# Where the steps of attention stand among the float16 and float32 passes of a gated block, and what follows them on the other engines

## The chip, the cores and the metric

The kernel runs on one core of a Trainium2 chip. The metric is the device time of the program in microseconds (us), as the median of several runs. TensorE (PE in the profile, its weight loads PEld), VectorE (DVE), ScalarE (ACT), GpSimd (POOL) and SyncE's DMA queue (SP) each work through a program of their own, in order, and wait for each other by semaphores.

## The reference

The input x has shape (8, 512, 256): eight batch elements of 512 tokens. After a layer norm, two branches read the same xn; the result is x + s * silu(f).

```python
x = L0_attn_query
xn = _layernorm(x, axis=-1)
s = _L0_attn_ref(xn, L0_attn_in_proj_w, L0_attn_out_proj_w)
g = _silu(_L0_ffn_ref(xn, L0_ffn_k0, L0_ffn_k1, L0_ffn_k2, L0_ffn_s0, L0_ffn_s1, L0_ffn_s2))
x = x + s * g
```

`_L0_attn_ref` has 16 heads of size 16: query, key and value projections, a rotary embedding of queries and keys, scores masked to the 250 latest positions (`(delta >= 0) & (delta < 250)`), softmax, values, and an output projection. `_L0_ffn_ref` has three layers whose weights are +1 or -1 (from booleans): [xn, -xn] of width 512 to 1024, relu and times 2, 1024 to 1024, relu and times 2, 1024 to 256. All of it is float32.

## The kernel before, in words

**Units.** The program handles the batch elements as eight units, b = 0 to 7, of T = 512 tokens in four tiles of 128. Work of neighbouring units overlaps: while unit b runs its feed-forward layers and its attention, unit b+1's norm, transposes (`turn_x`, tile `xnT_ps`) and key and query projections (`ka`, `kb`, `qa`, `qb`) are placed among them, and so are the third layer (`last`, `z_ps`) and the output projection of unit b-1.

**Two passes.** Each layer's product is made in two passes into one PSUM bank (`layer`, L396, matmuls L412): first "h", float16 weights and the float16 high part of the activations, then "l", float32 weights and the low part (`h1l`, `h2l`, type fp32r). Layer 1 is short (2 + 2 matmuls of 512 columns for each of 8 output tiles f), layer 2 long (8 + 8). ACT makes the high part with a relu (L423), DVE the low part from the PSUM bank (L421), and then the bank is free. In the last unit layer 2 is done in halves of 256 columns.

**Attention.** A unit's attention is nine steps (`steps`, L568, `step` and `attention`, L713). One step issues the score matmuls (`scores`, L598, each of 32 contraction rows), and behind them the value matmuls of the step before (`values`, L672, tile `po`). Between the two lie the exponentials on ACT, in two halves (L617), and the masks on POOL (`mask`, L633 and L640). When the heads of a group are complete, `keep` moves V and the sums S out of `po`: scalings on ACT for even groups (L692), additions on DVE for odd ones (L696). Group pairs are then divided: `invert` (DVE, reciprocals of S in four quarters, L742), `divide` (a DVE shuffle to R, L748, a product V*R on POOL, L751, and a count of unfit sums on POOL and DVE, L755 and L760).

**The end of a unit.** `gate_ready` (L492) makes 1/(1+exp(-z)): an exponential on ACT (L495), +1 on POOL (L498), a reciprocal on DVE (L502), a product on POOL (L503). `project_o` (L766) makes the output projection of tile t (`att_ps`, L770), issues the load of x's tile `xr` on SP (L775), multiplies by the gate on DVE (L783), adds xr on POOL and stores the result by a DMA on SP (L788, L789). `late` (L518) places `project_o`, and `gate_ready` comes 4 units of model time before it.

**What sets the order.** Everything is a list of pieces (time, cost, function). `run` (L209) sorts them by time and calls them; each may return followers with a delay, which go into a heap and are called when the sum of the costs so far has reached their due time. The order of the calls is the program order on every engine. The times are a model: SEQ = 42.0 for a unit, L1 = 0.87 for one f of layer 1, L2 = 3.45 for one f of layer 2, L3 = 1.87 for a tile of the third layer. The second exponential comes 0.3 after the first, the masks 1.2 after that, or at the latest when the next step needs them. `attention` places the nine steps: among the pieces of the unit, in order of time, it takes the first one at which at least n/9 of the unit's cost is done, and puts step n just ahead of it. Two pieces of one f of layer 2 (its h pass and its l pass) have times of their own, so a step can come to stand between the passes.

**PSUM.** Scores use 2 tiles of two banks, `po` one bank, and all else shares three banks (`ps_m`), which go round in program order. `probs`, the exponentials, has two buffers.

In a steady unit of the kernel before, TensorE's order is, with "sc po" for a step (scores of step n, values of step n-1) and h/l for the passes:

```
h1.0 v0 h1.1 v1 z0 sc1 po v2 v3 ... h1.5 z.2 sc2 po h1.6 h1.7 z.3 h2.0h sc3 po h2.0l xnT0 h2.1h xnT1 xnT2 h2.1l
sc4 po xnT3 h2.2h ka h2.2l kb sc5 po h2.3h qa qb h2.3l sc6 po h2.4h h2.4l att0 h2.5h sc7 po h2.5l att1
h2.6h h2.6l sc8 po att2 h2.7h h2.7l att3 sc0 po
```

Of the kernel before, what the change touches and what calls it, by code (L numbers as in the profile page):

```python
# [34 lines left out]
def tile_attention_times_gated_ffn(  # L35
# [39 lines left out]
    B, T, E = x.shape  # L75
# [123 lines left out]
    SEQ = 42.0  # L199
    L1, L2, L3 = 0.87, 3.45, 1.87  # L200
    states = {}

    def warm():

# [191 lines left out]
    def layer(b, name, src, w, f, part=0, parts_=1, cols=slice(0, T)):  # L396

        st = states[b]
        nc_in = w["l"].shape[1]
        if f == 0 and part == 0 and cols.start == 0:  # L400
            for p, dt in (("h", F16), ("l", F32R)):
                st[name + p] = hpool.tile(
                    [P, NF0, T], dt, tag=f"{name}{p}", name=f"{name}{p}_{b}"
                )
        if part == 0:
            st["h"] = ps_m.tile([P, T], F32, tag="mm", name=f"h_ps_{b}_{f}")
        ph = st["h"][:, cols]
        of_both = [(p, c) for p in "hl" for c in range(nc_in)]
        n = len(of_both)
        for k in range(n * part // parts_, n * (part + 1) // parts_):  # L410
            p, c = of_both[k]
            nc.tensor.matmul(  # L412
                ph, w[p][:, c, ts(f, P)], st[src + p][:, c, cols],
                start=(k == 0), stop=(k == n - 1),
            )
        if part + 1 < parts_:
            return
        hi, lo = (st[name + p][:, f, cols] for p in "hl")

        def low():  # L420
            nc.vector.scalar_tensor_tensor(lo, ph, 0.0, hi, ALU.max, ALU.subtract)  # L421

        high = lambda: nc.scalar.activation(hi, ph, AF.Relu)  # L423
        return [(0.0, high), (0.6 if f + 1 < NF0 else 0.0, low)]

    def last(b, t, how):
        st = states[b]
        pz = ps_m.tile([P, E], F32, tag="mm", name=f"z_ps_{b}_{t}")
        if how == "at once":
            for c in range(NF1):  # L430
                nc.tensor.matmul(
                    pz, st["h2p"][:, c, ts(t, P)], w2["l"][:, c].bitcast(F32),
                    start=(c == 0), stop=(c == NF1 - 1),
                )
        else:
            for p in "hl":
                for c in range(NF1):
                    nc.tensor.matmul(  # L438
                        pz, st["h2" + p][:, c, ts(t, P)], w2[p][:, c],
                        start=(c == 0 and p == "h"), stop=(c == NF1 - 1 and p == "l"),  # L440
                    )
        gate = st["gate", t] = outs.tile([P, E], F32, tag=f"gate{t}", name=f"gate_{b}_{t}")
        if how == "final":
            den = denominator(b, t)

            def ends():
                nc.scalar.activation(den, pz, AF.Exp, scale=scales[:, 1:2])
                nc.vector.scalar_tensor_tensor(
                    gate, pz, scales[:, 0:1], st["att", t], ALU.mult, ALU.mult
                )  # L450
                return [(0.5, add)]

            def add():
                nc.scalar.activation(den, den, AF.Identity, bias=1.0)
                return [(0.4, final)]

            def final():
                nc.vector.reciprocal(den, den)
                nc.vector.tensor_tensor(gate, gate, den, ALU.mult)
                nc.vector.tensor_tensor(gate, gate, st["xr", t], ALU.add)  # L460
                nc.sync.dma_start(out[b, ts(t, P), :], gate)

            return [(0.0, ends)]

        def scale():
            nc.vector.tensor_scalar(gate, pz, scales[:, 0:1], None, ALU.mult)
            if how != "later":
                return [(0.5, lambda: gate_ready(b, t))]

        return [(0.0, scale)]  # L470
# [40 lines left out]
    def last_at(b, t):  # L511

        if b + 1 < B:
            return SEQ * (b + 1) + 2 * L1 * (t + 1) + L3 * t
        half = t // 2
        return SEQ * b + NF0 * L1 + NT * L3 + HALF * (half + 1) - 2 * L3 + L3 * (t % 2)

    def late(b, t):  # L518

        if b + 1 == B:  # L520
            return SEQ * b + 40.0 + 0.9 * t
        return SEQ * (b + 1) + (31.0 + 3.5 * t if b + 2 < B else 18.0 + 2.5 * t)

    def finish_ffn(b, t, how):
        out = [(last_at(b, t), L3, lambda: last(b, t, how))]
        if how == "later":
            out.append((late(b, t) - 4.0, 0, lambda: gate_ready(b, t)))
        return out

    def ffn(b):  # L530

        now = SEQ * b + (NT * L3 if b == 0 else 0)
        out = []
        for f in range(NF0):
            out.append((now, L1, lambda f=f: layer(b, "h1", "x", w0, f)))
            now += L1
            if f % 2 and b > 0:
                now += L3
        if b + 1 == B:
            for half in range(2):  # L540
                cols = ts(half, T // 2)
                for f in range(NF1):
                    out.append((
                        now, L2 / 2,
                        lambda f=f, cols=cols: layer(b, "h2", "h1", w1, f, cols=cols),
                    ))
                    now += L2 / 2
                now += 2 * L3
            return out
        for f in range(NF1):  # L550
            for i in range(2):
                out.append(
                    (now, L2 / 2, lambda f=f, i=i: layer(b, "h2", "h1", w1, f, i, 2))
                )
                now += L2 / 2
        return out
# [11 lines left out]
    steps = [  # L568
        [(0, *whole_0), (0, *left_1)],
        [(0, *right_1), (0, *whole_2)],  # L570
        [(0, *whole_3), (1, *whole_0)],
        [(1, *whole_1), (1, *whole_3)],
        [(1, *whole_2), (2, *whole_2)],
        [(2, *whole_0), (2, *left_1)],
        [(2, *right_1), (2, *whole_3), (3, *whole_3)],
        [(3, *whole_0), (3, *left_1)],
# [5 lines left out]
    def once(f):  # L582

        calls = [f]
        return lambda: calls.pop()() if calls else None
# [23 lines left out]
    def exponentials(b, i, sc, n):  # L609
        p = probs.tile([P, 4, T], F32, tag="p", name=f"p_{b}_{i}")  # L610

        def exps():
            half_of(0)
            return [(0.3, second)]

        def half_of(half):
            nc.scalar.activation(  # L617
                p[:, 2 * half : 2 * half + 2, :n], sc[half][:, :, :n], AF.Exp,
                scale=D ** -0.5,
            )  # L620

        second = once(lambda: half_of(1) or [(1.2, masks)])
        masks = once(lambda: mask(i, p))
        return p, lambda: (second(), masks()), once(exps)

# [87 lines left out]
    def attention(b, among):  # L713

        first, end = SEQ * b + (20.6 if b == 0 else 0.0), ends_at(b)
        inside = sorted((at, cost) for at, cost, _ in among if first <= at < end)
        whole = sum(cost for _, cost in inside)
        times, done = [], 0.0
        for at, cost in inside:
            if len(times) < len(steps) and done * len(steps) >= whole * len(times):  # L720
                times.append(at - 0.01)
            done += cost
        out = []
        for n in range(len(steps)):
            out.append((times[n], 1.7, lambda n=n: step(b, n)))
        for g in range(NG):

            at = times[used[g - 2][-1]] + 0.01 if g > 1 else first - (10.0 if b else 2.0)
            if b and g == 1:
                at = first + 0.01  # L730
            out.append((at, 0, lambda g=g: stack(b, g)))
        if b + 1 == B:
            out.append((end, 0.7, flush))
        return out
# [65 lines left out]
    def divisions(b):  # L800
        out = []
        for pair in range(2):
            if b + 1 < B:
                first, d = (SEQ * b + 29.0, 2.0) if pair == 0 else (SEQ * (b + 1) + 4.2, 2.0)
            else:
                first, d = SEQ * b + (20.0 if pair == 0 else 30.6), 1.3
            for n in range(4):
                out.append((first + d * n, 0, lambda p=pair, n=n: invert(b, p, n)))
            out.append((first + d * 4, 0, lambda p=pair: divide(b, p)))
        return out  # L810

    whole = small.tile([1, 1], mybir.dt.int32, tag="whole", name="whole")
# [169 lines left out]
```

## Time and profile before

| what | value |
|---|---|
| median of three runs | 635.44 us (634.3 to 636.73) |
| the profiled execution | 636.03 us, span 634.3 us |
| granted TensorE clock, mean | 0.993 |
| TensorE busy | 612.7 us, 97% of the span |
| VectorE, GpSimd, ScalarE busy | 388.8, 312.3, 297.7 us |
| starts of units 0 to 7 on TensorE (first matmul of layer 1) | 19.03, 91.31, 166.61, 242.04, 317.33, 393.02, 468.59, 544.43 us |
| last matmul of the body | about 624.5 us |

The page has one line for each engine's busy time, a row of tenths for forty slices of the span, the chain of work that ended last, and groups of instructions by line. A timeline lists an engine's instructions by start, with their duration, and in brackets the engine's idle time ahead of one and what ended it. [...] a matmul group's bar reaches into the next one's; what a piece costs TensorE is read from its start to the next piece's start. A unit's period is the distance of two unit starts.

### The profile page before, as it was taken

How to read it: one execution, taken by the hardware profiler on the slowest of the kernel's cores; microseconds unless marked ns; L12 is line 12 of the kernel's file. 1: busy time of each engine (PE TensorE's matmuls, PEld its weight loads, DVE VectorE, ACT ScalarE, POOL GpSimd, SP SyncE). 2: the span in 40 equal slices, each digit the busy share in tenths (PEclk: the TensorE clock that was granted, in tenths of full speed). 3: DMA queues.
4: the chain of work that ended last, by engine and by line, in shares of the span. 5: the costliest groups of instructions: out<-in, count | busy, mean ns of one | idle time of the engine just before them, and what ended most of it. 6: DMA issues, size and time to landing. Idle time of an engine off the chain costs nothing.

```text
span 634.3 us, 12013 instructions
## 1 busy us (share of the span) xinstructions
PE 612.7 (97%) x4834; PEld 398.8 (63%) x4834; DVE 388.8 (61%) x668; ACT 297.7 (47%) x442; POOL 312.3 (49%) x406
## 2 busy tenths in 40 slices
PE   7899999999999999999999999999999999999993
PEld 5454567656766567655676566665666556768783
DVE  6584436656675475756657577665566557457564
ACT  3566564525444445444454454452545445464321
POOL 1935451455633557426544348145472346738630
PEclk9899999999999999999999999999999999999998
DMA  8263621215321153113431153311443115221101
GB/s 270 78 232 117 233 85 34 63 71 177 123 85 50 68 208 126 51 51 146 145 109 51 63 197 106 116 62 76 151 127 105 51 68 208 93 85 42 52 25 40
DMA packets 38194, 67.21 MB, mean 106 GB/s; under 512 B 5104, under 2 KB 19184, under 8 KB 38128
## 3 DMA queue, kind: packets, MB, share of 16 engines
q1 hardware_dynamic: 36384, 64.24, 29.7%
q10 hardware_dynamic: 1744, 2.10, 1.0%
q8 instruction: 40, 0.66, 0.4%
q14 instruction: 26, 0.21, 0.1%
HBM read 36.96 MB, written 29.36 MB: 105 GB/s over the span
## 4 chain that ended last, share of the span: by engine, by line
PE 70%; POOL 8%; DVE 6%; DMA 5%; ACT 5%; issue 3%; SPq 1%; POOLq 0%; ACTq 0%
PE h_ps L412 32%; PE z_ps L438 8%; PE po L672 8%; PE sc L598 6%; PE v_ps L289 4%; DMA xr<-in_x_dram 3%; PE att_ps L770 3%; ACT p L617 2%; DMA kb<-in_k_dram 2%; PE kb_ps L304 2%; PE ka_ps L304 2%; PE qb_ps L304 1%; PE qa_ps L304 1%; DVE den L502 1%; PE xnT_ps L265 1%
## 5 line engine op out<-in xcount | busy, mean ns | idle before, releaser
L617 ACT ACTIVATE p<-sc 128x1024 f32<-128x1024 f32 (+2 forms) x144 | 138.5, 1014 | 119.0 <-PE sc L598 80.9
L412 PE MATMUL h_ps<-h1l,w1l_sb 128*128 128x512 f32 (+1 forms) x576 | 143.1, 390 | 0.0
L633 POOL TENSOR_SCALAR_AFFINE_SELECT p<-p 128x512 f32<-128x512 f32 x128 | 88.0, 693 | 76.2 <-ACT p L617 76.1
L412 PE MATMUL h_ps<-h1h,w1h_sb 128*128 128x512 f16 (+1 forms) x576 | 122.8, 356 | 0.9 <-ACT v_pad L296 0.5
L412 PEld LDWEIGHTS h_ps<-h1l,w1l_sb 128*128 128x128 f32 x576 | 98.4, 188 | 27.6 <-issue 9.6
L423 ACT ACTIVATE h2h<-h_ps 128x512 f16<-128x512 f32 (+1 forms) x72 | 39.9, 554 | 113.8 <-PE h_ps L412 113.7
L412 PEld LDWEIGHTS <-w1h_sb 128*128 128x128 f16 x576 | 53.6, 98 | 52.3 <-issue 7.5
L672 PE MATMUL po<-p,v_pad 128*32 128x378 f32 (+4 forms) x1216 | 76.9, 372 | 1.7 <-POOL p L640 1.3
L502 DVE RECIPROCAL den<-den 128x256 f32<-128x256 f32 x30 | 52.2, 1739 | 41.5 <-POOL den L498 41.5
L421 DVE SCALAR_TENSOR_TENSOR h2l<-h_ps,h2h 128x512 fp32r<-128x512 f32 (+1 forms) x72 | 43.5, 605 | 43.0 <-ACT h2h L423 43.0
L640 POOL TENSOR_SCALAR_AFFINE_SELECT p<-p 128x512 f32<-128x512 f32 (+1 forms) x96 | 49.2, 512 | 41.2 <-ACT p L617 41.1
L421 DVE SCALAR_TENSOR_TENSOR h1l<-h_ps,h1h 128x512 fp32r<-128x512 f32 x64 | 42.6, 676 | 33.4 <-ACT h1h L423 33.1
L598 PEld LDWEIGHTS sc<-q,k 32*128 32x128 f32 x1216 | 44.0, 184 | 28.4 <-issue 18.8
L742 DVE RECIPROCAL S<-S 128x128 f32<-128x128 f32 x64 | 59.3, 934 | 0.0
L598 PE MATMUL sc<-q,k 32*128 32x378 f32 (+4 forms) x1216 | 57.1, 306 | 0.0
L412 PE MATMUL h_ps<-xl,w0l_sb 128*128 128x512 f32 x128 | 53.5, 500 | 0.0
L423 ACT ACTIVATE h1h<-h_ps 128x512 f16<-128x512 f32 x64 | 38.2, 597 | 32.6 <-PE h_ps L412 32.3
L672 PEld LDWEIGHTS po<-p,v_pad 128*32 128x32 f32 x1216 | 31.7, 109 | 30.7 <-issue 16.7
L788 POOL TENSOR_TENSOR gate<-gate,xr 128x256 f32<-128x256 f32 x30 | 22.0, 732 | 51.0 <-DMA xr<-in_x_dram 38.6
L412 PE MATMUL h_ps<-xh,w0h_sb 128*128 128x512 f16 x128 | 39.5, 391 | 0.6 <-DVE gate L783 0.5
L438 PE MATMUL z_ps<-w2l_sb,h2l 128*128 128x256 f32 x256 | 38.3, 291 | 0.5 <-DVE h2l L421 0.5
L336 POOL TENSOR_TENSOR m_ka<-m_ka,m_kb 128x512 f32<-128x512 f32 x16 | 20.1, 1278 | 34.3 <-DVE m_kb L316 31.8
(95 smaller groups left out, 809.5 us busy)
## 6 DMA issues: line engine op xcount, KB each, us to landing
q<-dq SPq DMA_DIRECT2D x64, 256.0 KB, 3.5
dq<-qh SPq DMA_DIRECT2D x16, 512.0 KB, 3.4
dq<-m_qa SPq DMA_DIRECT2D x16, 512.0 KB, 3.8
k<-dk SPq DMA_DIRECT2D x32, 256.0 KB, 2.7
dk<-kh SPq DMA_DIRECT2D x8, 512.0 KB, 2.6
dk<-m_ka SPq DMA_DIRECT2D x8, 512.0 KB, 2.6
xr<-in_x_dram SPq DMA_DIRECT2D x32, 128.0 KB, 2.9
out_dram<-gate SPq DMA_DIRECT2D x32, 128.0 KB, 1.7
```

Source lines behind the costliest of these rows:

```text
L304: nc.tensor.matmul(ps, wqkv_sb[:, c, ds(col, P)], st["xT"][:, c, :], start=(c == 0), stop=(c == EC - 1),)
L412: nc.tensor.matmul(ph, w[p][:, c, ts(f, P)], st[src + p][:, c, cols], start=(k == 0), stop=(k == n - 1),)
L421: nc.vector.scalar_tensor_tensor(lo, ph, 0.0, hi, ALU.max, ALU.subtract)
L423: high = lambda: nc.scalar.activation(hi, ph, AF.Relu)
L438: nc.tensor.matmul(pz, st["h2" + p][:, c, ts(t, P)], w2[p][:, c], start=(c == 0 and p == "h"), stop=(c == NF1 - 1 and p == "l"),)
L502: nc.vector.reciprocal(den, den)
L598: nc.tensor.matmul(sc[r // 2][:, r % 2, ds(off, n)], st["k0", g][row, ts(j, P)], st[f"q{turn}", g][row, ds(j * P + first, n)], start=(turn ...
L617: nc.scalar.activation(p[:, 2 * half : 2 * half + 2, :n], sc[half][:, :, :n], AF.Exp, scale=D ** -0.5,)
L633: nc.gpsimd.affine_select(out=block, in_=block, compare_op=ALU.is_ge, fill=0.0, base=0, pattern=[[0, 4], [1, P]], channel_multiplier=-1,)
L640: nc.gpsimd.affine_select(out=block, in_=block, compare_op=ALU.is_ge, fill=0.0, base=-1, pattern=[[0, 4], [-1, beyond]], channel_multiplier=1,
L672: nc.tensor.matmul(po[32 * r : 32 * r + 32, ds(j * P + first, n)], v_columns(j, g, r), p_[:, r, ds(off, n)], start=(j == 0), stop=(done an ...
L742: nc.vector.reciprocal(part, part)
```

## The change

Four edits, none of which adds or removes an instruction on any engine:

1. A set `quick` collects the times of the pieces whose first pass is float16: each third-layer tile, each f of layer 1, and each f of layer 2 as a whole (for the last unit each half of an f). `attention` now places step n ahead of that one of these pieces whose share of the unit's cost is nearest to n/9; each place is used once. In unit 0 every piece is allowed.
2. `late` for units 0 to 5 goes from 31.0 + 3.5 t to 32.0 + 3.2 t, for the output projections and, 4 earlier, `gate_ready`.
3. The masks follow the second exponential by 0.6 in place of 1.2.
4. The divisions of the first pair start at 30.0 in place of 29.0.

```diff
+    quick = set()
...
-        return SEQ * (b + 1) + (31.0 + 3.5 * t if b + 2 < B else 18.0 + 2.5 * t)
+        return SEQ * (b + 1) + (32.0 + 3.2 * t if b + 2 < B else 18.0 + 2.5 * t)
 
     def finish_ffn(b, t, how):
+        quick.add(last_at(b, t))
...
         for f in range(NF0):
+            quick.add(now)
             out.append((now, L1, lambda f=f: layer(b, "h1", "x", w0, f)))
...
                 for f in range(NF1):
+                    quick.add(now)
                     out.append((
                         now, L2 / 2,
                         lambda f=f, cols=cols: layer(b, "h2", "h1", w1, f, cols=cols),
...
         for f in range(NF1):
+            quick.add(now)
             for i in range(2):
                 out.append(
                     (now, L2 / 2, lambda f=f, i=i: layer(b, "h2", "h1", w1, f, i, 2))
...
-        second = once(lambda: half_of(1) or [(1.2, masks)])
+        second = once(lambda: half_of(1) or [(0.6, masks)])
...
         times, done = [], 0.0
+        places = {}
         for at, cost in inside:
-            if len(times) < len(steps) and done * len(steps) >= whole * len(times):
-                times.append(at - 0.01)
+            if at in quick or b == 0:
+                places[at] = done
             done += cost
+        for n in range(len(steps)):
+            at = min(places, key=lambda at: abs(places[at] * len(steps) - whole * n))
+            del places[at]
+            times.append(at - 0.01)
...
-                first, d = (SEQ * b + 29.0, 2.0) if pair == 0 else (SEQ * (b + 1) + 4.2, 2.0)
+                first, d = (SEQ * b + 30.0, 2.0) if pair == 0 else (SEQ * (b + 1) + 4.2, 2.0)
```

In a steady unit this gives, on TensorE:

```
h1.0 v0 h1.1 v1 z0 sc1 po v2 v3 ... h1.5 sc2 po z.2 h1.6 h1.7 z.3 sc3 po h2.0h h2.0l xnT0 h2.1h xnT1 xnT2 h2.1l
xnT3 sc4 po h2.2h ka h2.2l kb sc5 po h2.3h qa qb h2.3l sc6 po h2.4h h2.4l sc7 po h2.5h att0 h2.5l
h2.6h att1 h2.6l att2 sc8 po h2.7h h2.7l att3 sc0 po
```

Steps 2, 3, 4, 7 and 8 stand elsewhere, and the output projections of tiles 0 and 1 stand between the passes of h2.5 and h2.6. In the last unit steps 2 to 6 stand up to a piece earlier. POOL's order at the end of a unit changes from `den_2+1, gate_1+xr_1, gate_2*den_2, den_3+1, masks of step 8, gate_2+xr_2, V*R` to `den_2+1, gate_1+xr_1, gate_2*den_2, den_3+1, gate_2+xr_2, V*R, masks of step 8`, and on SP the loads of the next unit's first stack (one of k, two of q) stand ahead of the store of tile 0. In the last unit DVE's reciprocal of den_1 stands ahead of the V and S additions.

## The prediction

> **What bounds the kernel now.** I read the page first, then the windows by unit, then the timelines of TensorE and of all engines in units 2 and 3. The busy row and the chain that ended last:
>
> ```profile
> PE 612.7 (97%) x4834; PEld 398.8 (63%) x4834; DVE 388.8 (61%) x668; ACT 297.7 (47%) x442; POOL 312.3 (49%) x406
> ...
> PE 70%; POOL 8%; DVE 6%; DMA 5%; ACT 5%; issue 3%; SPq 1%; POOLq 0%; ACTq 0%
> ```
>
> TensorE is busy 97% of 634.3 us and no other engine above 61%. The units start at 19.03, 91.31, 166.61, 242.04, 317.33, 393.02, 468.59 and 544.43. Windows cut there (columns: length, then busy us and count of PE, weight loads, DVE, ACT, POOL, then granted clock, DMA share, GB/s):
>
> ```profile
> 242.04:317.33 75.29, 75.15 (x589) 47.89 (x585) 48.20 (x81) 35.26 (x53) 36.61 (x50) 1.00 0.32 105
> ...
> 544.43:634.30 89.87, 78.31 (x758) 62.63 (x754) 51.27 (x85) 35.55 (x62) 40.70 (x55) 0.97 0.18 55
> ```
>
> Units 1 to 6 are TensorE end to end: 453.1 us for six, the shortest 75.29. Only the order of TensorE's work, and short waits, can move them. "Busy" hides the second part, since the bars overlap, so I measured from start to start. TensorE in unit 2:
>
> ```profile
> 223.11 1.89 PE L412 MATMUL h_ps<-h1h,w1h_sb 128*128 128x512 f16 x8
> 224.93 0.79 PE L598 MATMUL sc<-q,k 32*128 32x378 f32 x16
> 225.65 0.84 PE L672 MATMUL po<-p,v_pad 128*32 128x244 f32 x16
> 226.42 2.14 PE L412 MATMUL h_ps<-h1l,w1l_sb 128*128 128x512 f32 x8
> 228.40 1.02 PE L770 MATMUL att_ps<-wo_sb,V 128*128 128x256 f32 x4
> 229.26 1.89 PE L412 MATMUL h_ps<-h1h,w1h_sb 128*128 128x512 f16 x8
> 230.79 2.21 PE L412 MATMUL h_ps<-h1l,w1l_sb 128*128 128x512 f32 x8
> 232.94 0.74 PE L598 MATMUL sc<-q,k 32*128 32x244 f32 x16
> ```
>
> An unbroken pair of passes followed by a step takes 232.94 − 229.26 = 3.68 us. The pair with step 7 inside takes 228.40 − 223.11 = 5.29, less 0.72 for scores and 0.77 for values = 3.80. A step inside a pair costs 0.12 more than one in front of a float16 pass.
>
> The third view is the only sizeable wait that repeats. All engines in unit 3, after step 3 (stood inside a pair):
>
> ```profile
> 266.55 1.92 ACT L617 ACTIVATE p<-sc 128x1012 f32<-128x1012 f32 x2 [3.78 <-PE sc L598]
> ...
> 269.49 0.62 ACT L423 ACTIVATE h2h<-h_ps 128x512 f16<-128x512 f32 x1
> ...
> 270.14 0.69 DVE L421 SCALAR_TENSOR_TENSOR h2l<-h_ps,h2h 128x512 fp32r<-128x512 f32 x1 [0.23 <-ACT h2h L423]
> ...
> 270.89 0.20 PEld L265 LDWEIGHTS xnT_ps<-ident,xn 128*128 128x128 f32 x2 [0.59 <-DVE h2l L421]
> ```
>
> ACT is in the exponentials of step 3 and two scalings when the layer-2 product ends, so the relu comes late, the residual on DVE after it, and the transpose that needs the PSUM bank waits. From h pass to transpose is 1.983 us here; without such a wait it is 1.727. Cost 0.26 a unit.
>
> [...] the page's weight-load groups show 98 ns for w1h (float16), 188 ns for w1l. [...] In the trace the long load is hidden after 512-column matmuls (an f16 pass to its l pass has no extra time), but not after values: from values to the second matmul of an l pass is 0.34 us against 0.23 elsewhere. [...] the relu stands behind exponentials.
>
> **The change part by part.** Instruction counts on each engine stay, so everything is order. PE, DVE and POOL programs were read in both versions.
>
> *Steps in steady units (1 to 6).* Steps 2, 3, 4, 7 and 8 move. Boundary prices, start to start: values before an l pass +0.11, before a transpose +0.055, before an output projection (att) +0.107 (0.968 against 0.861), before a float16 pass 0; before scores always about 0.10, whatever stands there. Step 2 moves from one float16 pass (h1) to another (z): 0. Step 3 leaves the inside of pair 0: −0.116. Step 4 moves from a transpose to h2.h2: −0.03 after small shifts. Step 7 leaves pair 5 and step 8 moves behind att 2: the stretch from step 7 to att 3 is 14.20 now; the pieces in the new order sum to 14.01: −0.19. Sum −0.34 a unit.
>
> *Output projection one unit of model time later.* Att 0 and 1 now stand inside pairs 5 and 6. The nearest row is the projection ka inside a pair: 200.86 to 206.16 is 5.30, which is an unbroken pair in front of att 3 (235.80 to 239.38, 3.58) plus qa's own advance (1.72). So a float32 piece there costs 0; bounds 0 and +0.11 each. I take 0, since the full-width load behind a 512-column matmul is hidden in that row.
>
> *Transpose wait.* Step 3 now ends a whole pair before the relu that it delayed, so ACT is free: −0.26 a unit (bounds 0 and −0.26). The stall could move to step 4, now before h2.h2, but that relu is one pair off: 0.
>
> *Small waits.* Six units at the floor of 75.20 would be 451.2, so 1.93 us are stray waits (the v copies and step-8 masks). I leave 1.2, or 0.2 a unit. Together: 6 × (−0.34 − 0.26) − 0.73 = −4.3.
>
> *Masks sooner, divisions later, and the queues.* POOL's order changes at each unit's end. Before:
>
> ```profile
> 312.69 0.73 POOL L788 TENSOR_TENSOR gate<-gate,xr 128x256 f32<-128x256 f32 x1 [3.39 <-DMA xr<-in_x_dram]
> ...
> 314.89 0.64 POOL L640 TENSOR_SCALAR_AFFINE_SELECT p<-p 128x512 f32<-128x512 f32 x1
> ```
>
> Step 8's masks stood behind the gate_1+xr_1 store and ended at 316.29, just when values needed them. After, they stand behind gate_2+xr_2 and V·R, too. On SP the three loads of the next unit's first stack go ahead of out_0, so xr_1 is issued about 304.6 (was 308.80). Then in unit 3: xr_1 lands 308.5, sum to 309.2, out_1, xr_2 issued 309.6, landed 312.0 (2.4, as for xr_2 before), sum 312.7, V·R (1.28) 314.0, masks (1.4) 315.4. Values want them at 316.0. Cover 0.6 us. I cost it at 0, but if xr_2 takes 3.9, as xr_1 did, it is +0.9 a unit. Mask of step 6 likewise: its exponentials end 295.8, den_0's exponential now stands ahead of them on ACT, masks end about 297.7, values at 298.4. Att 3's product, behind masks on POOL, is ready about 316.5 and its bank is wanted at 318.8.
>
> *Unit 0.* Steps 2, 3, 7, 8 move: −0.15. Scores to values of step 4 take 1.08 against 0.67 for lack of masks (0.4); these come 0.6 sooner: −0.35. Sum −0.5.
>
> *Last unit.* Waits now: 0.92 (step 8's values, 0.86 of it masks behind two gate sums), and about 1.6 around the z passes and flush (masks, h2l). After, steps 2 to 6 stand one piece sooner, and on DVE den_1's reciprocal (1.75) moves ahead of the V and S scalings that step 6's values need. In sequence: masks of step 4 from 569.2, V·R 1.28, den_0+1 0.85, reciprocal 1.75, product 0.74, den_1+1 0.85, reciprocal 1.75, V and S 1.5, so values at about 580.0 with TensorE there at 578.4: +1.6. Behind it, part of the later waits disappears (0.9 + 0.4, and transitions 0.3). Sum 0, bounds −1 and +1.5.
>
> *Sum.* −4.3 − 0.5 + 0 = −4.8 on the profiled execution's 636.03: 631.2. The median shown is 0.59 below it, so 630.6. Start and tail (19.0 us before unit 0, 9.7 after TensorE's last matmul) are left as they are.
>
> **Rivals.**
> *The likeliest* ends at 629.4 to 632.0: boundaries and the transpose pay, the rest nearly cancels.
> *Given back in part*: att inside pairs costs 0.1 each (+1.2 in six units), or the last unit shows its 1.5 in full: 632 to 634.5. For it: the DVE row den is 1.74 us[...]. Against: ka in a pair costs nothing.
> *More*: masks and xr stay early in the last unit and its 0.9 plus 0.9 fall away: 628 to 629.4. For it, POOL is 49% busy; against, den_1 on DVE.
> *Slower*: the POOL queue at the unit's end. If xr_2 lands 1.5 us or more later than I set (the page has 2.9 median, 5.6 at most), step 8's masks hold up step 0's values in seven units. Past the 0.6 cover it costs one for one; at 0.7 a unit the gain is gone, at 1.2 it is 639.0. For it: 38.6 us of POOL's idle time ended on xr. Against: out_0 and so xr_1 go sooner.
> *No effect*: pairs cost the same whatever they surround, the 0.12 being where records start; the transposes' wait moves to another bank: 635.
>
> **How the numbers follow.** The chances: likeliest 0.60, given back 0.18, more 0.12, slower 0.06, no effect 0.04. Half a per cent is 3.2 us, about what a measurement of this kernel can tell from no change: bounds 632.3 and 638.6. Faster: 0.60 + 0.12 + 0.04 of the second = 0.76. Same: 0.14 + 0.04 = 0.18. Slower 0.06. The range 628.0 to 634.2 takes in the first three but their ends and leaves out the last two.
>
> **What would show it.** Right: units 1 to 6 at 74.6 to 74.9; the pair with step 7 gone from TensorE's timeline and its pairs at 3.68 between att and scores; h pass to transpose 1 at 1.73, with the relu at its product's end. Wrong: TensorE idle on p from POOL L640 in front of step 0's values in steady units, with V·R or gate+xr ahead of the masks; values at 0.1 or more longer before att; units at 75.2; and a wait over 1.6 us at step 6 of the last unit.

## The result, and the profile after

The changed kernel takes 630.84 us as the median of four runs (630.22 to 632.4), the kernel before 635.39 (634.3 to 636.73) beside it: a ratio of 0.992, with a 95% interval of 0.990 to 0.9941. The forecast was 630.6. The profiled execution of the changed kernel took 632.4 us with a span of 630.6, so the two profiled executions differ by 3.6 us.

The busy row and the chain of work that ended last, of the changed kernel:

```profile
PE 609.6 (97%) x4834; PEld 398.8 (63%) x4834; DVE 393.0 (62%) x668; ACT 300.0 (48%) x442; POOL 316.1 (50%) x406
...
PE 84%; DVE 6%; DMA 4%; POOL 3%; ACT 2%; issue 1%; SPq 0%; POOLq 0%; ACTq 0%
```

TensorE is as busy as before, but its share of the last chain rose from 70% to 84%, and POOL's fell from 8% to 3%: fewer waits in front of TensorE end at POOL (its waits for masks fell from 1.3 us, in three, to 0.3, in two). The units start at 19.03, 90.63, 166.20, 241.24, 316.15, 391.06, 465.92 and 540.84, and the last matmul of the body ends at 620.31 (before: 624.54). Windows of the changed kernel for units 3 and 7 (columns as in the prediction: length, then busy us and count of PE, weight loads, DVE, ACT, POOL, then granted clock, DMA share, GB/s):

```profile
241.24:316.15 74.91, 74.77 (x588) 47.95 (x585) 48.85 (x82) 35.64 (x53) 38.66 (x51) 1.00 0.32 106
...
540.84:630.60 89.76, 77.91 (x758) 62.44 (x754) 51.07 (x84) 35.53 (x62) 39.87 (x54) 0.97 0.17 54
```

| stretch | before | after | difference | forecast |
|---|---|---|---|---|
| unit 0 | 72.28 | 71.60 | -0.68 | -0.5 |
| units 1 to 6, sum | 453.13 | 450.21 | -2.92 | -4.3 |
| unit 7, to the last matmul | 80.11 | 79.47 | -0.64 | 0 |
| after the last matmul | 9.76 | 10.29 | +0.53 | 0 |
| span | 634.3 | 630.6 | -3.7 | -4.8 |

TensorE in unit 2 of the changed kernel, at the place where step 7 stood inside a pair:

```profile
221.71 0.82 PE L605 MATMUL sc<-q,k 32*128 32x378 f32 x16
222.45 0.84 PE L679 MATMUL po<-p,v_pad 128*32 128x244 f32 x16
223.22 1.90 PE L415 MATMUL h_ps<-h1h,w1h_sb 128*128 128x512 f16 x8
224.96 1.03 PE L782 MATMUL att_ps<-wo_sb,V 128*128 128x256 f32 x4
225.63 2.21 PE L415 MATMUL h_ps<-h1l,w1l_sb 128*128 128x512 f32 x8
227.68 1.90 PE L415 MATMUL h_ps<-h1h,w1h_sb 128*128 128x512 f16 x8
```

The pair with att 0 inside takes 227.68 − 223.22 = 4.46 us, an unbroken pair's 3.58 plus 0.88. So the projection costs its own time there and nothing more, as forecast.

All engines of the changed kernel in unit 3, at the transpose that was forecast to lose its wait:

```profile
267.89 0.60 ACT L426 ACTIVATE h2h<-h_ps 128x512 f16<-128x512 f32 x1 [0.88 <-PE h_ps L415]
267.91 1.89 PE L415 MATMUL h_ps<-h1h,w1h_sb 128*128 128x512 f16 x8
268.11 0.42 DVE L280 COPY xT<-xnT_ps 128x256 f32<-128x256 f32 x1 [0.79 <-PE xnT_ps L268]
268.45 0.79 DVE L250 TENSOR_SCALAR xn<-x,mv,rstd 128x256 f32<-128x256 f32 x1
...
269.17 0.68 DVE L424 SCALAR_TENSOR_TENSOR h2l<-h_ps,h2h 128x512 fp32r<-128x512 f32 x1
...
269.90 0.20 PEld L268 LDWEIGHTS xnT_ps<-ident,xn 128*128 128x128 f32 x2 [0.59 <-DVE h2l L424]
```

ACT is now free and takes the relu as soon as the product ends, as forecast: in step with the next h pass, where it came 0.58 us behind it before. But the transpose still waits: 269.90 − 267.91 = 1.99 us, as before (1.98). The residual h2l could have started at the earliest when the relu ended, at 268.49. It starts at 269.17, because the norm of the next tile (0.79 us) stands ahead of it on DVE. It stood there before, too, where it ended ahead of the relu; the h pass and the norm of the kernel before:

```profile
268.91 1.89 PE L412 MATMUL h_ps<-h1h,w1h_sb 128*128 128x512 f16 x8
...
269.45 0.46 DVE L247 TENSOR_SCALAR xn<-x,mv,rstd 128x256 f32<-128x256 f32 x1
```

POOL of the changed kernel at the end of unit 3:

```profile
311.88 0.74 POOL L800 TENSOR_TENSOR gate<-gate,xr 128x256 f32<-128x256 f32 x1 [1.34 <-DMA xr<-in_x_dram]
312.58 1.28 POOL L763 TENSOR_TENSOR V<-V,R 128x512 f32<-128x512 f32 x1
313.81 0.64 POOL L647 TENSOR_SCALAR_AFFINE_SELECT p<-p 128x512 f32<-128x512 f32 x1
...
314.99 0.23 POOL L647 TENSOR_SCALAR_AFFINE_SELECT p<-p 128x24 f32<-128x24 f32 x1
```

Step 8's masks end at 315.22, and the values of step 0 start at 315.17. The forecast's times for this unit were on the clock of before, where the unit starts at 242.04; here it starts at 241.24. From the start of the unit the values come at 73.93 us (forecast 73.96), but the masks end at 73.98 (forecast 73.36). The cover of 0.6 us doesn't exist: the masks come just in time. In unit 1, where xr_2 came later, step 0's values waited, and scores to unit end took 0.58 us more (0.95 and 1.34 against 0.73 and 0.98).

### The profile page after: what moved, and what is told of

It reads as the page before. It is cut to its first block, busy times and chain, and to the rows that moved or that the text cites. A ratio compares the mean times of both kernels' runs of the same rounds, so it can differ in the third digit from the quotient of the medians.

```text
span 630.6 us, 12029 instructions
## 1 busy us (share of the span) xinstructions
PE 609.6 (97%) x4834; PEld 398.8 (63%) x4834; DVE 393.0 (62%) x668; ACT 300.0 (48%) x442; POOL 316.1 (50%) x406
## 4 chain that ended last, share of the span: by engine, by line
PE 84%; DVE 6%; DMA 4%; POOL 3%; ACT 2%; issue 1%; SPq 0%; POOLq 0%; ACTq 0%
PE h_ps L415 40%; PE po L679 11%; PE z_ps L441 9%; PE sc L605 7%; PE v_ps L292 4%; PE att_ps L782 4%; PE qa_ps L307 2%; PE kb_ps L307 2%; PE qb_ps L307 2%; DMA kb<-in_k_dram 2%; DMA xr<-in_x_dram 2%; PE ka_ps L307 2%; PE xnT_ps L268 1%; DVE den L505 1%; ACT p L624 1%
## 5 line engine op out<-in xcount | busy, mean ns | idle before, releaser
L640 POOL TENSOR_SCALAR_AFFINE_SELECT p<-p 128x512 f32<-128x512 f32 x128 | 93.8, 739 | 106.5 <-ACT p L624 106.5
L415 PEld LDWEIGHTS <-w1h_sb 128*128 128x128 f16 x576 | 51.6, 98 | 55.8 <-issue 14.0
```

Source lines behind the costliest of these rows:

```text
L415: nc.tensor.matmul(ph, w[p][:, c, ts(f, P)], st[src + p][:, c, cols], start=(k == 0), stop=(k == n - 1),)
L640: nc.gpsimd.affine_select(out=block, in_=block, compare_op=ALU.is_ge, fill=0.0, base=0, pattern=[[0, 4], [1, P]], channel_multiplier=-1,)
```

## The experiments

One table for all; units are those of the profile of each run, the ratio is to the runs of the kernel before on the same chip.

| kernel | units 2 to 6, us | unit 7 to last matmul, us | median, us | ratio (95% interval) |
|---|---|---|---|---|
| before | 75.29 to 75.85 | 80.11 | 635.39 | 1 |
| changed | 74.86 to 75.04 | 79.47 | 630.84 | 0.992 (0.990 to 0.9941) |
| edit 1 (places) alone | 76.94 to 79.59 | 78.27 | 649.63 | 1.0212 (1.0184 to 1.024) |
| edit 2 (projection later) alone | 75.24 to 75.25 | 80.10 | 634.03 | 0.9983 (0.9974 to 0.9991) |
| edit 3 (masks sooner) alone | 75.76 to 77.11 | 83.09 | 643.76 | 1.0139 (1.0118 to 1.016) |
| edit 4 (divisions later) alone | 75.20 to 76.10 | 80.72 | 635.43 | 1.0 (0.9992 to 1.0009) |
| edits 1 and 2 | 74.90 to 75.19 | 78.28 | 631.27 | 0.9931 (0.9915 to 0.9948) |
| edits 1 and 3 | 76.33 to 77.88 | 79.42 | 642.71 | 1.0109 (1.0086 to 1.0132) |
| changed, xn edit | 74.69 | 79.45 | 629.06 | 0.9902 (0.988 to 0.9925) |
| before, xn edit | 75.22 to 75.99 | 80.27 | 635.46 | 1.0001 (0.999 to 1.0012) |
| changed, steps 3 to 7 inside pairs | 76.80 to 77.64 | 79.44 | 642.71 | 1.0101 (1.0075 to 1.0128) |
| edit 1, xr loaded early | 74.87 to 74.89 | 78.27 | 629.3 | 0.9901 (0.9875 to 0.9928) |
| changed, xn edit, last masks as before | 74.70 | 78.29 | 628.39 | 0.9881 (0.9858 to 0.9903) |
| edit 1, xr early, xn edit | 74.71 | 78.28 | 628.75 | 0.9893 (0.9873 to 0.9914) |

The theory after the result: the boundaries give about 0.33 us a unit; the other edits matter only for stray waits; the transpose's wait moved from ACT to DVE. The rival: the queues carry the change, edits 2 and 3 above all.

### Each edit alone

Edit 1 alone, which is the changed kernel with these three undone:

```diff
-        return SEQ * (b + 1) + (32.0 + 3.2 * t if b + 2 < B else 18.0 + 2.5 * t)
+        return SEQ * (b + 1) + (31.0 + 3.5 * t if b + 2 < B else 18.0 + 2.5 * t)
...
-        second = once(lambda: half_of(1) or [(0.6, masks)])
+        second = once(lambda: half_of(1) or [(1.2, masks)])
...
-                first, d = (SEQ * b + 30.0, 2.0) if pair == 0 else (SEQ * (b + 1) + 4.2, 2.0)
+                first, d = (SEQ * b + 29.0, 2.0) if pair == 0 else (SEQ * (b + 1) + 4.2, 2.0)
```

> The kernel before with edit 1 alone (the places of the steps). Theory (the boundary prices carry the gain): units 2 to 6 at 74.9 us against 75.3 to 75.85, as in the changed kernel, ratio about 0.994 (3.5 to 4 us). Rival (the queue edits carry it: the later output projection, the sooner masks): units stay at 75.2 or more, since masks or the gate chain stall, ratio 0.997 or above.

Measured: 14 us slower than before, on the rival's side and far beyond its 0.997. Against the theory the units are 2 to 5 us too long. POOL of the kernel with edit 1 alone, at the end of unit 3:

```profile
309.75 0.73 POOL L800 TENSOR_TENSOR gate<-gate,xr 128x256 f32<-128x256 f32 x1 [4.28 <-DMA xr<-in_x_dram]
...
316.83 0.72 POOL L800 TENSOR_TENSOR gate<-gate,xr 128x256 f32<-128x256 f32 x1 [3.09 <-DVE h2l L424]
...
320.22 0.72 POOL L800 TENSOR_TENSOR gate<-gate,xr 128x256 f32<-128x256 f32 x1 [1.15 <-DMA xr<-in_x_dram]
320.90 1.27 POOL L763 TENSOR_TENSOR V<-V,R 128x512 f32<-128x512 f32 x1
322.13 0.72 POOL L506 TENSOR_TENSOR gate<-gate,den 128x256 f32<-128x256 f32 x1
322.81 0.63 POOL L647 TENSOR_SCALAR_AFFINE_SELECT p<-p 128x512 f32<-128x512 f32 x1
```

and its TensorE there:

```profile
320.68 0.79 PE L605 MATMUL sc<-q,k 32*128 32x378 f32 x16
323.50 1.85 PE L679 MATMUL po<-p,v_pad 128*32 128x244 f32 x16 [2.03 <-POOL p L647]
325.28 1.03 PE L415 MATMUL h_ps<-xh,w0h_sb 128*128 128x512 f16 x2
```

Step 8's masks stand behind three sums with xr, V*R and gate 3's product. POOL waits for xr_0 for 4.28 us, and the whole chain of loads and sums is late by the time step 8's masks come up. This is the prediction's "slower" rival, in the place that it named, in each of the units 1 to 6 (in all, TensorE waits 11.3 us for masks).

The wait is also dearer than its length. Windows of two microseconds of the same kernel, in which the last columns are granted clock, DMA share and GB/s:

```profile
321.40:323.50 2.10, 0.07 (x5) 0.00 (x1) 0.42 (x1) 1.90 (x2) 2.10 (x4) 1.00 0.40 125
323.50:325.50 2.00, 1.85 (x17) 0.49 (x18) 0.09 (x1) 0.03 (x1) 1.92 (x3) 0.70 0.00 0
325.50:327.50 2.00, 2.00 (x6) 1.45 (x5) 2.00 (x3) 0.30 (x1) 1.92 (x4) 0.50 0.01 4
327.50:329.50 2.00, 2.00 (x10) 1.55 (x9) 0.93 (x3) 0.88 (x3) 1.31 (x2) 0.95 0.86 243
```

After the idle 2.1 us the trace shows a granted clock of 0.5 for 3.41 us, from 324.28 on. In starts: the values take 1.78 in place of 0.98. After the like wait in unit 6, at full clock, they take 1.34: the last mask comes late too (here it ends at 324.21) and holds up their second half. So of the 0.80 here 0.36 is a second wait and 0.44 the clock. At the start of unit 3, after the wait at the end of unit 2, the first matmul groups and v projections took 1.54 more than usual. So unit 3 pays 4.4 us, 2.5 for its waits and 2.0 for the clock, and 74.88 + 4.4 is its period of 79.31 (rounding aside).

Edit 2 alone is the `late` line of the change in the kernel before.

> The kernel before with edit 2 alone (output projections and gates one unit of model time later). Theory: att 0 and att 1 stand inside pairs and cost only themselves there, step 7 still stands inside pair 5: boundaries sum to 0, units 75.1 to 75.6, ratio 0.998 to 1.002. Rival (the later projection by itself saves the waits at the unit's end): units at 75.2 without exception and the last unit 1 us shorter, ratio 0.996 or below.

Measured: 0.17% faster, in the theory's span of ratios. The unit periods are the rival's: 75.24 or 75.25 in units 2 to 6. The later projection takes away the stray waits, and leaves the last unit (80.10) as it was.

Edit 3 alone is the 0.6 in place of the 1.2.

> The kernel before with edit 3 alone (masks 0.6 in place of 1.2 after the second exponential). TensorE's order is that of before. Theory: unit 0 loses its 0.4 us in front of step 4's values and some stray waits go, no more: 0.5 to 1 us in all, ratio about 0.999. Rival (masks were the hidden bound, POOL being late everywhere): 2 us or more, ratio 0.997 or below.

Measured: 8 us slower; both theories failed. In the traces TensorE, DVE, ACT and SP have the order of before and POOL alone another, so the masks' places on POOL are the cause, shown by the run itself. The units are up to 1.5 us longer (0.25 to 0.76 between step 8's scores and values in five of six, and waits at the units' starts), the last unit 3.0. Which piece behind the masks costs what was not taken apart.

Edit 4 alone is the 30.0 in place of the 29.0.

> The kernel before with edit 4 alone (first pair's divisions 1 later). Theory: reciprocals of S move on DVE where nothing waits for them, 0: ratio 1.000 within 0.001. Rival: V*R comes later on POOL and so lets step 8's masks or gate 2 through, the waits at the units' starts (0.2 to 0.6 us each in units 2, 4, 6) go, 1 to 1.5 us, ratio 0.998.

Measured: 1.0, as the theory says; the waits at the starts stay.

### Which edit makes edit 1 pay

Edits 1 and 2, then edits 1 and 3, each as in the change and without the other two.

> Edits 1 and 2 together, without 3 and 4. With edit 1 alone units 2 to 5 took 78.6 to 79.6 us, with step 0's values waiting about 2 us for step 8's masks. Theory (the order around the first projection decides): with edit 2 POOL no longer waits for xr_0 in front of step 7's masks and gate 1's product, so the chain of loads and sums of xr starts early; only gate 3's product (0.72) still stands ahead of step 8's masks, so 0 to 0.5 us of wait: units 74.9 to 75.4, ratio 0.992 to 0.996. Rival (the sooner masks are needed as well): units 77 us or more, ratio above 1.005.

> Edits 1 and 3 together, without 2 and 4. Step 8's masks move ahead of gate 3's product on POOL (0.72), but stay behind gate_2+xr_2 and V*R, and gate_0+xr_0 stays in front. Theory: the wait at step 0's values falls from about 2.2 to 1.5 us and stays: units 76.5 to 78.5, ratio 1.005 to 1.018. Rival (the masks' place is the whole matter): units at 75, ratio 0.993.

Measured: with edit 2 the units fall to 74.90 to 75.19 and the ratio to 0.9931, inside the theory; with edit 3 they stay at 76.33 to 77.88 and the ratio at 1.0109, as the theory there has it within 0.2 us. So edit 2 is enough to make edit 1 pay and edit 3 is not; edits 1 and 4 together were not run. With edit 2 POOL does step 7's masks and gate 1's product ahead of the sum with xr_0. The two kernels show a third thing: with edits 1 and 2 the last unit takes 78.28 us, 1.2 less than in the changed kernel.

To see whether it is the loads of xr that hold POOL up, edit 1 alone was run with each load issued at the gate's start, into four buffers in place of two:

```diff
+    def load_xr(b, t):
+        xr = states[b]["xr", t] = work.tile(
+            [P, E], F32, tag="xr", name=f"xr_{b}_{t}", bufs=4
+        )
+        nc.sync.dma_start(xr, x[b, ts(t, P), :])
+
     def gate_ready(b, t):
         st = states[b]
+        if b + 1 < B:
+            load_xr(b, t)
...
-        xr = work.tile([P, E], F32, tag="xr", name=f"xr_{b}_{t}")
-        nc.sync.dma_start(xr, x[b, ts(t, P), :])
-        st["xr", t] = xr
+        if b + 1 == B:
+            load_xr(b, t)
+        xr = st["xr", t]
```

> Edit 1 alone, as in the first run, but with the load of xr issued at the gate's start, 4 units of model time ahead of the projection, into four buffers. TensorE's and POOL's order are those of the first run. Theory (POOL stands still for xr_0 and xr_1, whose loads stand behind stores on SP, and step 8's masks are late for that): the waits for xr go, step 0's values wait 0 to 0.7 us, units 74.9 to 75.8, ratio 0.992 to 0.998. Rival (the chain of gate, reciprocal and sums on POOL and DVE is too long by itself): units at 77 or more, ratio above 1.005.

Measured: 629.3 us, 20 us less than edit 1 alone. In the traces TensorE, POOL, DVE and ACT do the same work in the same order; only SP's order and the buffers differ. POOL of this kernel in unit 3, at the sums with xr_0, xr_1 and xr_2:

```profile
297.15 0.72 POOL L808 TENSOR_TENSOR gate<-gate,xr 128x256 f32<-128x256 f32 x1
...
302.74 0.73 POOL L808 TENSOR_TENSOR gate<-gate,xr 128x256 f32<-128x256 f32 x1
...
306.97 0.73 POOL L808 TENSOR_TENSOR gate<-gate,xr 128x256 f32<-128x256 f32 x1
```

None waits, and no unit waits at its end. The theory's cause holds, and the gain is larger than it said (0.9901 against 0.992 to 0.998, units of 74.87 to 74.89 against 74.9 to 75.8): with edit 1 alone POOL stood still for loads (4.28 us for xr_0 in unit 3), which stood behind stores and other loads on SP (xr_1, issued at 312.34, behind the store of tile 0 at 310.50 and the loads of k and q). With the loads early, edit 1 needs none of the other three.

### The transpose's wait

The xn edit: a third buffer (in the last unit `att` shares it), and the norm of tile 2 right behind that of tile 1, ahead of the first transpose's copy on DVE.

```diff
-        xn = st["xn", t] = work.tile([P, E], F32, tag="xn", name=f"xn_{b}_{t}")
+        xn = st["xn", t] = work.tile([P, E], F32, tag="xn", name=f"xn_{b}_{t}", bufs=3)
...
-                (at["norm"] + dx * t, 0, lambda t=t: norm(b, t)),
+                (at["norm"] + (1.9 if b and t == 2 else dx * t), 0, lambda t=t: norm(b, t)),
...
-            att = st["att", t] = work.tile([P, E], F32, tag="xn", name=f"att_{b}_{t}")
+            att = st["att", t] = work.tile([P, E], F32, tag="xn", name=f"att_{b}_{t}", bufs=3)
```

> The changed kernel with a third buffer for xn and the norm of tile 2 placed before the first transpose's copy, so that on DVE it no longer stands between the relu of layer 2's f = 0 and its residual. Theory (in the changed kernel the transpose waits for DVE's queue, which stood hidden behind ACT before): from the h pass to transpose 1 takes 1.73 in place of 1.99 us, units 74.6 to 74.7, about 1.5 us less than the changed kernel, ratio to the kernel before about 0.990. Rival (the wait is the bare chain of relu, residual and transpose): 1.99 stays and so does the time.

> The kernel before with the same edit to xn as in the run above and nothing else. Theory (there ACT's exponentials and scalings make the relu late and DVE is ready in time): from the h pass to transpose 1 stays at 1.98 us, units as before, 0 us. Rival (DVE is the cause in both kernels): 1.73 here too, 1.5 us less.

Measured: 1.73 us from h pass to transpose in all six units on the changed kernel, and units of 74.69; on the kernel before 1.98 in all six, and no change in time. Both theories hold. All engines of the changed kernel with the xn edit, unit 3:

```profile
265.76 0.60 ACT L426 ACTIVATE h2h<-h_ps 128x512 f16<-128x512 f32 x1 [0.88 <-PE h_ps L415]
...
266.39 0.69 DVE L424 SCALAR_TENSOR_TENSOR h2l<-h_ps,h2h 128x512 fp32r<-128x512 f32 x1
...
267.30 0.58 PEld L268 LDWEIGHTS xnT_ps<-ident,xn 128*128 128x128 f32 x4
```

The residual follows the relu at once, and the weight load for the transpose is there before the h pass ends, without a wait. So the wait had two causes in a row: ACT in the kernel before, with DVE's behind it, and DVE's alone in the changed one.

The unit gains less than the wait suggests. In unit 3 the first transpose comes 0.26 sooner and the second no longer waits behind it (0.26 more), but the transpose of tile 3, 1.95 us behind its l pass in the changed kernel, now comes 2.30 behind it, since it waits for DVE to empty its PSUM bank:

```profile
270.17 0.41 PE L268 MATMUL xnT_ps<-ident,xn 128*128 128x128 f32 x2 [0.19 <-DVE xl L284]
```

The period falls from 74.91 to 74.69, by 0.17 us here and 0.05 in small shifts.

### The price of a boundary

Steps 3 to 7 put inside their pairs:

```diff
-            times.append(at - 0.01)
+            times.append(at - 0.01 + (L2 / 2 if 0 < b < B - 1 and 2 < n < 8 else 0.0))
```

> The changed kernel with steps 3 to 7 of units 1 to 6 put between the two passes of their pairs on purpose; step 8 and all else as in the changed kernel. Theory (the price is 0.116 us for values in front of a float32 pass with 128 weight columns): five steps times 0.116 = 0.58 us a unit, units 75.4 to 75.6 against 74.9, 3 to 4 us in all, ratio to the kernel before about 0.997. Rival (the 0.12 read from starts is only where records begin): units stay at 74.9, ratio 0.992.

Measured: units of 76.80 and more, three times the loss expected. Unit 3 (76.80 against 74.91) splits like this: the last z pass to h2.0 takes 2.05 in place of 1.03, so a wait of 1.02; transpose 3 to h2.2 0.42 in place of 0.22, 0.20; a v projection 0.15. What is left is 0.52 for five steps, 0.10 each, near the 0.116. For step 3 alone it can be read from the starts: its pair, scores, values and the z pass ahead take 5.90 us without the wait, against 5.78, so 0.12. The rival falls, but most of the loss is the wait, which TensorE of this kernel shows:

```profile
264.76 0.75 PE L441 MATMUL z_ps<-w2l_sb,h2l 128*128 128x256 f32 x5
266.37 1.89 PE L415 MATMUL h_ps<-h1h,w1h_sb 128*128 128x512 f16 x8 [0.86 <-DVE h1l L424]
```

The first pair's bank is released by layer 1's last residual but one, which starts at 265.69 on DVE, behind the next unit's statistics and a reciprocal of S (262.28 to 265.77). In the changed kernel step 3 stands in front of that pair, and its 1.08 us (scores 0.72, values 0.36) cover the wait.

### The last unit

In the changed kernel the values of step 6 wait, as forecast. TensorE of the changed kernel, unit 7:

```profile
573.92 0.90 PE L605 MATMUL sc<-q,k 32*128 32x244 f32 x24
575.93 1.50 PE L679 MATMUL po<-p,v_pad 128*32 128x378 f32 x24 [1.11 <-DVE S L703]
```

and its DVE:

```profile
572.80 1.75 DVE L505 RECIPROCAL den<-den 128x256 f32<-128x256 f32 x1 [1.07 <-POOL den L501]
574.47 0.65 DVE L703 SCALAR_TENSOR_TENSOR V<-po,s_sb,V 128x512 f32<-128x512 f32 x1
575.04 0.74 DVE L703 SCALAR_TENSOR_TENSOR S<-po,s_sb,S 128x512 f32<-128x512 f32 x1
```

With edits 1 and 2 alone that unit is 1.2 us shorter. The difference is edit 3: it puts step 4's masks, which wait for exponentials, ahead of V*R (1.28) on POOL. POOL of the changed kernel, idle for 3.78 us ahead of the masks:

```profile
565.68 0.64 POOL L640 TENSOR_SCALAR_AFFINE_SELECT p<-p 128x512 f32<-128x512 f32 x1 [3.78 <-ACT p L624]
...
567.24 1.28 POOL L763 TENSOR_TENSOR V<-V,R 128x512 f32<-128x512 f32 x1
```

and of the kernel with edits 1 and 2, where V*R goes first:

```profile
564.38 1.27 POOL L763 TENSOR_TENSOR V<-V,R 128x512 f32<-128x512 f32 x1 [2.25 <-DVE R L760]
565.92 0.64 POOL L640 TENSOR_SCALAR_AFFINE_SELECT p<-p 128x512 f32<-128x512 f32 x1 [0.27 <-POOL V L763]
```

The run: the changed kernel with the xn edit, and in the last unit the masks as before.

```diff
-        second = once(lambda: half_of(1) or [(0.6, masks)])
+        second = once(lambda: half_of(1) or [(0.6 if b + 1 < B else 1.2, masks)])
```

> The changed kernel with the xn edit of the seventh run, and the masks of the last unit again 1.2 after the exponential (0.6 in units 0 to 6). On POOL the product V*R of the last unit then stands ahead of step 4's masks and not behind them. Theory (these masks hold up V*R, which holds up den_0, den_1 and DVE in front of step 6's values): the last unit takes 78.3 in place of 79.5 us, about 628 us in all, ratio about 0.988. Rival (the last unit's gain with edits 1 and 2 alone came from elsewhere): 79.5 as before, 629.

Measured: 78.29 us for the last unit, 628.39 in all, ratio 0.9881: the theory. The gain of edits 1 and 2 there is 1.8 us over the kernel before, and edit 3 gave two thirds of it back.

### A version without edits 2 to 4

Edit 1, the early loads and the xn edit together:

> Edit 1, the early load of xr into four buffers, and the xn edit; edits 2, 3 and 4 left out. Theory (three separate matters: boundaries 0.3 us a unit, the xr loads, the transpose's wait 0.25 us): steady units 74.6 to 74.7 with none that waits at its end, last unit 78.3, about 627.5 us, ratio about 0.987. Rival (the later projection of edit 2 is worth something beside the early load): 629 or more.

Measured: the units as the theory has them (74.71, and no wait at their ends), the time 628.75, between the theory's 627.5 and the rival's 629. Its interval (0.9873 to 0.9914) overlaps that of the run before it (0.9858 to 0.9903), so these two aren't told apart; both are faster than the kernel before by about 1%, and the unit periods put both ahead of the changed kernel. Whether edit 2 is worth anything beside early loads stays open.

## Why the prediction was right or wrong

**The boundaries: right.** Forecast −0.34 a unit. Without stray waits a unit in the order of before is 75.22 (with the xn edit) or 75.24 (edit 2 alone) and one of the changed kernel 74.86 to 74.91: −0.31 to −0.38, and −0.37 (74.87 against 75.24) with edit 1 and early loads. The page of the changed kernel has the weight loads at the lengths of before, 98 ns for w1h and 188 for w1l. The run with steps inside pairs agrees with the price, at 0.10 to 0.12; that the price comes from the long load, not hidden behind values, is an estimate argued from starts (the forecast's 0.34 us against 0.23) and was not tested apart. One reading of the forecast is off: from step 7's scores to att 3 its own lines give 14.45 (224.93 to 239.38), not 14.20. The difference, which is what counts, holds: from h2.4 to att 3 the two orders take 20.73 and 20.56 in unit 2, −0.17 against −0.19.

**Att inside pairs: right.** 0.88 against 0.86.

**The transpose: wrong.** The step that failed is "Step 3 now ends a whole pair before the relu that it delayed, so ACT is free: −0.26 a unit". ACT did come free; the wait stayed, since "ACT is in the exponentials" named only the cause that ended last. In the trace of before the norm of tile 2 stood on DVE in front of the same residual (269.45 to 269.91), and hid behind the relu, which ended at 270.11. This is 1.5 us of forecast gain, and the steady units fell 1.4 short (−2.92 against −4.3). The runs with the xn edit bring the 0.26 at this place, and 0.17 to 0.23 a unit from unit 3 on, since another transpose then waits.

**The stray waits: right in sum, by luck in part.** Forecast 1.2 left of 1.93, from a floor of 75.20 that the forecast doesn't derive; with the 75.22 to 75.24 of the runs it was 1.7 to 1.8. Over six units the changed kernel has 450.21 − 6 × 74.88 = 0.93 left, 0.69 of it in unit 1. But "Cover 0.6 us" was wrong: it is about 0. Counted from the unit's start, xr_1 was issued at 63.7 us and not at 62.6, xr_2 at 68.2 and not at 67.6, and the masks were late by the same 0.6. The step that failed is "xr_1 is issued about 304.6".

**The slower rival: right mechanism, in a kernel that wasn't forecast.** Its price was set at one for one; in unit 3 of edit 1 alone 2.5 us of waits cost 4.4, through the clock. And its release was credited to SP's order alone; the run with edits 1 and 2 shows that the later projection does it, through SP's order and POOL's (step 7's masks ahead of the sum with xr_0), which were not taken apart. Edits 2 to 4 were costed near 0 as moves, one by one; edits 1, 2 and 3 are worth +14, −1.4 and +8 us alone, and −4.5 together with edit 4.

**Unit 0: as forecast** (−0.68 against −0.5): step 4's scores to values fell from 1.08 to 0.68, and the last values from 1.27 to 0.98. Both lie in one profile each, and unit 0 took 69.8 to 72.6 us in the other runs, so no more is made of it. Much of that scatter arises at the unit's start, where TensorE waits 1.2 to 2.3 us for m_qb from DVE. In five of the fourteen profiles, the kernel before and the changed one among them, a stretch of 3.41 us at half clock follows, and the unit takes 71.3 to 72.6; in the other nine it takes 69.8 to 71.0.

**The last unit: the mechanism right, two terms mis-sized.** The wait at step 6 was forecast at 1.6 and is 1.18 (2.01 against 0.83 from scores to values). Of the later waits 0.9 and 0.4 were to disappear; 0.93 (1.60 to 0.67 at step 8) and 0.74 (1.88 to 1.14 at the z pass) did.

**The sum: close by luck in part.** The median fell by 4.55 us, to within 0.3 of the forecast; the profiled execution fell by 3.6, where 4.8 was forecast for it. In the profiles 1.4 us of the steady units' gain stayed away, the last unit gave 0.64 and the stretch behind it took 0.53, where 0 was forecast for both. Units 2 to 6, at 74.86 to 75.04, lie at or just above the upper end of the 74.6 to 74.9 named as the sign of being right, and the sign of 1.73 us from h pass to transpose failed.

## What to carry to other kernels

When a wait is about to be removed, read the whole queue of the engine that comes next after the one named: here the norm on DVE, ready 0.2 us before ACT, kept the wait alive. A change of order on one engine is to be followed on the queues of all others, as far as the loads behind a store: the same nine places cost 14 us with the loads of xr late and win 6 with them early. Here the wait at the units' ends went by loading sooner, without moving what stands behind it. And a wait that is gone can come back in part a few pieces on, as at the transpose of tile 3.

## What was not expected of the hardware

After an idle stretch TensorE's granted clock could fall to 0.50, and how long the stretch was didn't decide it alone. From the start of unit 0 on, the fourteen profiles hold eighteen waits of TensorE of 1.56 us or more. The six of 2.09 to 2.73 us all had a stretch at half clock begin in them or soon after. Of the twelve of 1.56 to 2.05 us six had one (1.56, 1.70, 1.74, 1.97, 2.03 and 2.05) and six had none (1.63, 1.65, 1.73, 1.83, 1.91 and 2.04); shorter ones had none. With edit 1 alone, at the end of unit 1:

```profile
165.57 1.41 PE L679 MATMUL po<-p,v_pad 128*32 128x244 f32 x16 [1.56 <-POOL p L647]
...
167.27:170.68 3.41, 3.41 (x11) 2.32 (x9) 2.57 (x5) 0.97 (x2) 3.33 (x5) 0.50 0.26 70
```

and the changed kernel with the xn edit, in unit 0, where the clock stays at 1.00:

```profile
23.15 1.13 PE L292 MATMUL v_ps<-wqkv_sb,xT 128*128 128x256 f32 x4 [2.04 <-DVE m_qb L319]
...
23.00:25.00 2.00, 1.85 (x8) 1.25 (x8) 1.29 (x3) 0.37 (x1) 2.00 (x2) 1.00 0.00 0
25.00:27.00 2.00, 2.00 (x10) 1.45 (x10) 0.91 (x2) 1.78 (x3) 2.00 (x3) 1.00 0.01 4
```

What the half clock costs shows where the same values follow a wait with and without it, with edits 1 and 3 at the ends of units 3 (clock 1.00) and 5 (0.50 from 473.02 on):

```profile
319.00 1.41 PE L679 MATMUL po<-p,v_pad 128*32 128x244 f32 x16 [1.63 <-POOL p L647]
...
472.79 1.85 PE L679 MATMUL po<-p,v_pad 128*32 128x244 f32 x16 [1.97 <-POOL p L647]
```

Up to the last matmul each stretch at half clock lasts 3.41 us. Those with edit 1 alone begin at 23.91, 167.27, 245.78, 324.28, 402.79 and 481.29: the first two lie 42 times 3.413 us apart, the others 23 times each. A fixed grid of that step, on which the place of a wait counts beside its length, is an estimate from these six starts alone; no run tests it.
